# Merging the attention stage and the feed-forward stage of the first block into one hand-ordered stage

## The chip, the cores and the metric

The program runs on one core of one Trainium2 chip. The metric is device time in microseconds (us) from start to end of one launch, on the slowest core, which here is the only one; lower is better. The core has five engines that run beside each other, each with a queue that is worked off in order: TensorE (PE; its weight loads are shown as PEld), VectorE (DVE), ScalarE (ACT), GpSimd (POOL) and SyncE (SP), which issues most of the transfers. TensorE writes to PSUM, eight banks of 128x512 fp32; the others read PSUM or SBUF, except GpSimd, which here works on SBUF alone. An instruction that needs a result of another engine waits for a semaphore, and what is queued behind it waits too.

## What is computed

The reference is a chain of four blocks on x of shape 16x256x128, each with an attention part and a feed-forward part, both wrapped in a norm before, a norm after, and a residual sum. The change touches the first block only, and the norm that starts the second:

```
x = x + layernorm(L0_attn(layernorm(x)))
x = x + layernorm(L0_ffn(layernorm(x)))
...   # the second block starts from layernorm(x)

def L0_attn(x):            # Wq, Wk: 128x32, one head
    score = (x @ Wq) @ (x @ Wk).T / sqrt(32)
    score = where(tril, score, 0);  score = where(score != 0, score, float32.min)
    return softmax(score) @ (x @ (Wvdown @ Wvup))

def L0_ffn(x):             # int weights / 127, hidden width 384
    return (silu(x @ wg.T) * (x @ wu.T)) @ wd.T
```

A score that is exactly zero is masked as well, not only one above the diagonal. The layernorm here has no gain or bias: (x - mean) / sqrt(var + 1e-5).

## The kernel before

**Tiling.** The 16 sequences of 256 tokens are cut into eight groups of two sequences. A group's tokens lie in one tile of 128 partitions by four column blocks (NT = 4) by 128 features; x[g], for g from 0 to 7, stays in SBUF throughout. Matmuls need features on the partitions, so a normed tile is transposed by TensorE, four 128x128 blocks into one PSUM bank (`transposed`, L311), and copied to SBUF. All matmuls of this block are fp32; each appears in the trace as two records.

**Norms.** `stats` (L260, L262) gives mean and variance of four token blocks on VectorE; GpSimd turns the variance into 1/sqrt (L249 a scale and sum, L250 a power); `normed` (L269) applies both on VectorE, four instructions of 128x128. `residual` norms y in this way and adds it to x on GpSimd (L289).

**The attention stage** `stage_l0_attn` (L550 on) makes, per group: norm, transposes, q and k (L322, copied out by `k.copy`, which alternates between VectorE, L242, and ScalarE, L244), values, and per sequence b the scores of 256 queries by 256 keys in one bank. VectorE then multiplies by a 0/1 causal mask (L581), marks zeros with -2^100 (L583), adds the marks (L584), takes the row maximum, negated (L586), and scales it (L587). ScalarE takes the exponential with that maximum as bias and gives the row sum (L592). TensorE transposes the weights (L602), ScalarE copies them (L604), TensorE multiplies by the values, and VectorE divides by the sums (L605, L612). The result is normed and added to x.

**The feed-forward stage** `stage_l0_ffn` (L621 on) starts when the attention stage has issued all its groups. It converts the integer weights (L627), and per group makes norm, transposes, and for three blocks of 128 hidden units a gate matmul, an up matmul, a silu on ScalarE (L643) and a product on VectorE (L644); then the down matmuls, the residual, and the norm of the new x into z[g], which the second block reads.

**What sets the order.** Both stages are Python generators, woven by `interleave`: three groups at a time, a new one every four steps, in the attention stage; four at a time, every three steps, in the other. The framework's scheduler then reorders the instructions of these stages within their queues. `turns` (L378 on) is another weave, used by later stages: each item has a starting turn and moves one step per turn (up to three when it is behind), and under `manual_schedule` the queues keep the order of the source. PSUM is given out in rings by tag: `BANKS` has four rings of two banks each ("mm", "s", "o", "t"); later stages use one large ring.

**Loads.** All loads are issued on SP in the order of the source, each taking some 0.43 us to issue: x of group 0, the identity, x of groups 1 and 2, the attention weights with the causal mask (256 KB), the other x, fourteen constants, the feed-forward weights, the next block's weights.

Of the kernel before, what the change touches and what calls it, by code (L numbers as in the profile page):

```python
# [31 lines left out]

BANKS = {"mm": 2, "s": 2, "o": 2, "t": 2}
MAMBA_BANKS = {"s": 6, "o": 2, "mm": "s", "t": "s"}
RING_BANKS = {"s": 7, "o": 1, "mm": "s", "t": "s"}
NEG = -(2.0**100)

# [68 lines left out]
    return c  # L106


def causal01():

    q = np.arange(SEQ).reshape(2, P).T
    return (np.arange(SEQ)[None, None, :] <= q[:, :, None]).astype(np.float32)


def packs(i):

    out = {"const": constants(), "att": attention_constants()}
    a = out["l0"] = Pack()
    a.add("wq", i["L0_attn_Wq"])
    a.add("wk", i["L0_attn_Wk"])  # L120
    a.add("causal", causal01())
    a = out["l0v"] = Pack()
    a.add("down", i["L0_attn_Wvdown"].T)
    a.add("up", i["L0_attn_Wvup"])
# [66 lines left out]
def idle(n):  # L191

    for _ in range(n):
        yield


def bc(ap, axis, n):

    ap = ap.unsqueeze(axis)
    shape = list(ap.shape)  # L200
    shape[axis] = n
    return ap.to_broadcast(shape)
# [343 lines left out]
        return out  # L546


def stage_l0_attn(k, x, w, wv):
    nc, v = k.nc, k.nc.vector  # L550
    scale = 1.0 / math.sqrt(32.0)
    ps = k.ps("mm")
    k.mm(ps[:, :D], wv["down"], wv["up"])
    wfull = k.t([P, D], "wfull", 1)
    v.tensor_copy(wfull, ps[:, :D])

    def group(g):
        xn = yield from k.norm(x[g], "xn", 3)
        yield
        xT = k.transposed(xn, "xT", 3)  # L560
        yield
        qk = []
        for name in ("wq", "wk"):
            ps = k.ps("mm")
            k.mm(ps[:32, :], w[name], xT)
            t = k.t([32, GT], name + "T", 3)
            k.copy(t, ps[:32, :])
            qk.append(t)
        yield
        val = k.tokens(xT, wfull, "v", 3)  # L570
        es, sms = [], []
        for b in range(2):
            keys = slice(b * SEQ, (b + 1) * SEQ)
            s = k.ps("s")
            for t in range(2):
                q = qk[0][:, (2 * b + t) * P : (2 * b + t + 1) * P]
                k.mm(s[:, t * SEQ : (t + 1) * SEQ], q, qk[1][:, keys])


            sc = k.t([P, 512], "sc", 4)  # L580
            v.tensor_tensor(sc, s, w["causal"], ALU.mult)  # L581
            z = k.t([P, 512], "z", 2)
            v.tensor_scalar(z, sc, 0.0, NEG, ALU.is_equal, ALU.mult)  # L583
            v.tensor_tensor(sc, sc, z, ALU.add)  # L584
            nm = k.t([P, 2], "nm", 6)
            v.tensor_reduce(nm, sc.rearrange("p (t n) -> p t n", t=2), AX.X, ALU.max, negate=True)  # L586
            v.tensor_scalar(nm, nm, scale, None, ALU.mult)  # L587
            e = k.t([P, 512], "e", 4)
            sm = k.t([P, 2], "sm", 6)
            for t in range(2):  # L590
                sl = slice(t * SEQ, (t + 1) * SEQ)
                nc.scalar.activation(  # L592
                    e[:, sl], sc[:, sl], AF.Exp, bias=nm[:, t : t + 1], scale=scale, accum_out=sm[:, t : t + 1]
                )
            es.append(e)
            sms.append(sm)
            yield
        o = k.t([P, NT, D], "o", 3)
        for b in range(2):
            tp = k.ps("t")  # L600
            for j in range(4):
                nc.tensor.transpose(tp[:, j * P : (j + 1) * P], es[b][:, j * P : (j + 1) * P], k.c["ident"])  # L602
            eT = k.t([P, 512], "eT", 3)
            nc.scalar.copy(eT, tp)  # L604
            v.reciprocal(sms[b], sms[b])  # L605
            yield
            ps = k.ps("o")
            for t in range(2):
                for kb in range(2):
                    at = (2 * t + kb) * P  # L610
                    k.mm(ps[:, t * D : (t + 1) * D], eT[:, at : at + P], val[:, 2 * b + kb, :], kb == 0, kb == 1)
            v.tensor_tensor(  # L612
                o[:, 2 * b : 2 * b + 2, :], ps[:, : 2 * D].rearrange("p (t d) -> p t d", t=2), bc(sms[b], 2, D), ALU.mult
            )
            yield
        yield from k.residual(x[g], o)

    k.interleave([group(g) for g in range(NG)], 3, 4)


def stage_l0_ffn(k, x, w, then):  # L621

    v = k.nc.vector
    f = {}
    for name in ("gate", "up", "down"):
        f[name] = k.t([P, 384], "f_" + name, 1)
        v.tensor_scalar(f[name], w[name], float(np.float32(1.0 / 127.0)), None, ALU.mult)  # L627
    down = f["down"].rearrange("p (c n) -> p c n", c=3)

    def group(g):  # L630
        xn = yield from k.norm(x[g], "xn", 3)
        yield
        xT = k.transposed(xn, "xT", 3)
        yield
        h = k.t([P, 3, GT], "h", 3)
        for c in range(3):
            cols = slice(c * P, (c + 1) * P)
            gt = k.ps("s")
            k.mm(gt, f["gate"][:, cols], xT)
            u = k.ps("mm")  # L640
            k.mm(u, f["up"][:, cols], xT)
            sg = k.t([P, GT], "sg", 3)
            k.nc.scalar.activation(sg, gt, AF.Silu)  # L643
            v.tensor_tensor(h[:, c, :], u, sg, ALU.mult)  # L644
            yield
        y = k.tokens(h, down, "y", 3)
        yield
        yield from k.residual(x[g], y)
        yield
        yield from then(g)  # L650

    k.interleave([group(g) for g in range(NG)], 4, 3)


def stage_l1_attn(k, x, ws, rows, z, then):
# [1043 lines left out]
def program(ctx: ExitStack, tc: tile.TileContext, xin, dram, at, out):  # L1699
# [12 lines left out]
    def load(p, name, only=None, dt=F32):  # L1712

        got = {}
        for n, (a, width) in at[name].items():
            if only is not None and n not in only:
                continue
            src = dram[name][:, a : a + width]
            t = p.tile([src.shape[0], width], dt, tag=f"{name}_{n}", name=f"{name}_{n}")
            nc.sync.dma_start(out=t, in_=src)  # L1720
            got[n] = t
        return got
# [11 lines left out]
    for g in range(NG):  # L1734
        nc.sync.dma_start(out=x[g], in_=xin[2 * g : 2 * g + 2].rearrange("b (t p) d -> p (b t) d", p=P))
        if g == 0:
            const = load(base, "const", {"ident"})
        elif g == 2:
            l0, l0v = load(p0, "l0"), load(p0, "l0v")
    const.update(load(base, "const", set(at["const"]) - {"ident"}))  # L1740
    k = Ctx(tc, const, None, None)
    k.load = load
    k.mhalf = base.tile([P, P], F32, tag="mhalf", name="mhalf")
# [10 lines left out]
    def stage(name, side, fn, *args, banks=BANKS):  # L1754
        with phase(name, banks, side):
            fn(k, x, *args)

    l0f = load(p0, "l0f", dt=I32)
    pa = opened("wa", "left")
    l1 = [load(pa, f"l1_{i}") for i in range(4)]  # L1760
    k.dram = ctx.enter_context(tc.tile_pool(name="spill", bufs=1, space=bass.MemoryType.DRAM))
    pz = opened("z", "left")
    z = [pz.tile([P, NT, D], F32, tag=f"z{g}", name=f"z{g}") for g in range(NG)]
    stage("l0a", "left", stage_l0_attn, l0, l0v)
    stage("l0f", "left", stage_l0_ffn, l0f, lambda g: k.norm_to(z[g], x[g]))
    closed("w0")
    l2 = load(opened("wb", "right"), "l2")
    psoft = opened("soft", "right")
# [57 lines left out]
```

## Time and profile before

| | |
|---|---|
| median of 3 runs | 3084.61 us (3083.8 to 3086.37) |
| profiled execution, its own time | 3086.15 us |
| its span in the trace | 3084.4 us |
| mean granted TensorE clock | 0.944 |
| busy over the span | PE 2781.1 (90%), PEld 1871.6 (61%), DVE 2038.4 (66%), ACT 1540.9 (50%), POOL 1000.8 (32%) |
| first transposes of the attention stage | 9.37 us |
| first gate matmul of the feed-forward stage | 144.0 us |
| last down matmuls | until 225.15 us |
| first transposes of the second block | 242.8 us |

The first block is thus some 8% of the span. The profile page cuts the span into 40 slices of 77 us and gives the busy share of each in tenths; the first block is the first three of them, in which PE shows 7, 7, 8 and the granted clock 7, 6, 9, while most later slices show PE at 9. A busy PE is not PE at its peak: matmuls are pipelined, and a matmul at a lower granted clock is busy for longer. For throughput one reads how far the starts of successive matmuls lie apart. Durations of single instructions are read from the groups of instructions (busy time and mean of one) and the timeline (instructions in order of time, merged when alike, with the idle time before them and what ended it). Idle time of an engine that is not the bottleneck costs nothing.

### The profile page before, as it was taken

Reading aid. Unit: us, or ns where it says so; the run is one execution under the profiler, and the core shown is the slowest. Engines: PE = TensorE matmul, PEld = TensorE weight load, DVE = VectorE, ACT = ScalarE, POOL = GpSimd, SP = SyncE. Lnnn points to the kernel's source line nnn. Section 1 sums busy time; section 2 is a strip of 40 time slices with the busy share of each in tenths; the row PEclk is TensorE's granted clock in tenths of the full one; section 3 lists DMA queues with packets and bytes.
Section 4 is the critical chain, followed back from the end, with each engine's and each line's share of the span. In section 5 each row is a group of like instructions: output and inputs, shape, how many; then the busy total and the mean of one; then the engine's idle time right before and its main releaser. Section 6 shows DMA issues by size and latency. Waiting matters only on the chain. (4 is left out here: it accounts for less than half of the span.)

```text
span 3084.4 us, 58954 instructions
## 1 busy us (share of the span) xinstructions
PE 2781.1 (90%) x23500; PEld 1871.6 (61%) x23500; DVE 2038.4 (66%) x5480; ACT 1540.9 (50%) x3237; POOL 1000.8 (32%) x1318
## 2 busy tenths in 40 slices
PE   7788999999999599999968999799999699978798
PEld 4445677777777488888853444466666344435576
DVE  6677656465566889899866774566665577637442
ACT  2224645555555467677634666344443277742222
POOL 1244333333335400000033555422232466553232
PEclk7698999999999799999988999899999799989899
DMA  3000000000000000000010000000000000010000
GB/s 100 25 1 1 2 1 2 1 1 1 1 2 18 19 8 8 12 12 8 8 45 27 2 1 1 1 1 1 1 1 1 1 1 1 1 55 1 1 15 15
DMA packets 29291, 31.52 MB, mean 10 GB/s; under 512 B 7308, under 2 KB 20172, under 8 KB 28876
## 3 DMA queue, kind: packets, MB, share of 16 engines
q1 hardware_dynamic: 29016, 27.76, 3.0%
q8 instruction: 185, 3.03, 0.4%
q14 instruction: 90, 0.74, 0.1%
HBM read 23.55 MB, written 4.19 MB: 9 GB/s over the span
## 5 line engine op out<-in xcount | busy, mean ns | idle before, releaser
L249 POOL TENSOR_SCALAR ln_rs<-ln_mv 128x4 f32<-128x4 f32 x192 | 39.5, 206 | 923.5 <-DVE ln_mv L262 812.5
L445 DVE TENSOR_REDUCE at_nm<-ps_s 128x2 f32<-128x512 f32 (+1 forms) x384 | 238.2, 682 | 123.1 <-PE ps_s L322 123.1
L477 ACT ACTIVATE at_e<-ps_s 128x512 f32<-128x512 f32 x384 | 198.1, 604 | 93.4 <-PE ps_s L322 91.2
L1311 DVE TENSOR_TENSOR scan<-ps_s,lm 128x384 f32<-128x384 f32 x256 | 124.7, 550 | 143.1 <-PE ps_s L322 142.8
L483 POOL TENSOR_SCALAR_AFFINE_SELECT at_e<-at_e 128x1024 f32<-128x1024 f32 (+1 forms) x96 | 135.1, 1408 | 215.8 <-ACT at_e L477 215.5
L250 POOL TENSOR_TENSOR ln_rs<-ln_rs,mhalf 128x4 f32<-128x4 f32 x192 | 194.6, 1015 | 15.1
L774 DVE TENSOR_REDUCE l_max<-ps_s 128x3 f32<-128x384 f32 x256 | 124.1, 549 | 64.0 <-PE ps_s L322 64.0
L322 PE MATMUL ps_o<-my,meT 128*128 128x129 f32 x1024 | 145.2, 289 | 19.5 <-ACT mgot L1068 17.0
L322 PEld LDWEIGHTS ps_s<-l_w,mlp_h 128*128 128x128 f32 x1280 | 149.4, 192 | 18.8 <-issue 15.1
L322 PE MATMUL ps_s<-l1f_phi,mxT 128*128 128x256 f32 x512 | 141.5, 399 | 16.4 <-DVE mpart L930 16.4
L322 PEld LDWEIGHTS ps_o<-my,meT 128*128 128x128 f32 x1024 | 128.7, 196 | 37.8 <-ACT mgot L1068 22.6
L322 PE MATMUL ps_s<-km,qT 32*128 32x512 f32 x768 | 140.2, 661 | 12.1 <-POOL km L369 10.7
L322 PE MATMUL ps_s<-l_w,mlp_h 128*128 128x128 f32 x1280 | 150.2, 275 | 0.3
L322 PE MATMUL ps_s<-qm,kT 32*128 32x512 f32 x768 | 144.1, 656 | 5.2 <-DVE at_nm L445 5.0
L824 POOL TENSOR_SCALAR_AFFINE_SELECT e<-e 128x512 f32<-128x512 f32 x128 | 78.6, 635 | 178.5 <-ACT e L821 178.5
L322 PE MATMUL ps_o<-at_e,at_vm 128*32 128x128 f32 (+1 forms) x2048 | 122.6, 336 | 15.2 <-ACT at_oT L507 15.2
L322 PE MATMUL ps_mm<-mdisp,mxn 128*128 128x128 f32 x1024 | 128.0, 282 | 4.6 <-DVE mdisp L968 4.5
L322 PEld LDWEIGHTS ps_mm<-mdisp,mxn 128*128 128x128 f32 x1024 | 124.4, 198 | 7.5 <-DVE mdisp L968 6.2
L821 ACT ACTIVATE e<-ps_s 128x384 f32<-128x384 f32 x256 | 105.6, 513 | 39.7 <-PE ps_s L322 39.6
L322 PE MATMUL ps_s<-xT,l_w 128*128 128x512 f32 x256 | 119.3, 596 | 2.7 <-ACT mlp_h L709 2.7
L1049 ACT ACTIVATE lg<-lg,mless 128x256 f32<-128x256 f32 x256 | 116.4, 523 | 0.0
L322 PEld LDWEIGHTS <-b_ident 128*128 128x128 bf16 x640 | 49.8, 98 | 108.8 <-issue 98.9
(418 smaller groups left out, 6978.9 us busy)
## 6 DMA issues: line engine op xcount, KB each, us to landing
mw<-in_l1fw SPq DMA_DIRECT2D x16, 256.0 KB, 2.6
moe_w<-in_moe SPq DMA_DIRECT2D x16, 256.0 KB, 5.3
l_w<-in_l SPq DMA_DIRECT2D x10, 256.0 KB, 3.2
x<-in_x SPq DMA_DIRECT2D x8, 256.0 KB, 4.1
xs<-x SPq DMA_DIRECT2D x8, 256.0 KB, 2.0
slT<-xs SPq DMA_DIRECT2D x8, 256.0 KB, 2.6
out<-x SPq DMA_DIRECT2D x8, 256.0 KB, 2.3
l1f_phi<-in_l1f SPq DMA_DIRECT2D x1, 1024.0 KB, 6.8
```

The source lines that it names most:

```text
L249: g.tensor_scalar(out, in_, scale, eps, ALU.mult, ALU.add)
L250: g.tensor_tensor(out, out, self.mhalf[:, :n], ALU.pow)
L322: self.nc.tensor.matmul(out, lhsT=lhsT, rhs=rhs, start=start, stop=stop, skip_group_check=True)
L445: v_.tensor_reduce(nm[:, t, r, vs], s, AX.X, ALU.max, negate=True)
L477: nc.scalar.activation(e[:, r], s, AF.Exp)
L483: nc.gpsimd.affine_select(at, at, [[0, 4], [0, n], [1, P]], ALU.is_ge, 0.0, base=0, channel_multiplier=-1)
L774: v.tensor_reduce(mx[:, b, :, h, 16], s, AX.X, ALU.max, negate=True)
L821: nc.scalar.activation(e[:, h].rearrange("p j n -> p (j n)"), s[:, : 3 * P], AF.Exp)
L824: nc.gpsimd.affine_select(e[:, :, j, :], e[:, :, j, :], [[0, 4], [1, P]], ALU.is_ge, 0.0, base=0, channel_multiplier=-1)
L1049: nc.scalar.activation(at, at, AF.Exp, bias=less[n][:, t, b : b + 1])
L1311: v.tensor_tensor(m, s[:, : SEQ + P], lm[:, SCAN_HEADS[4 * (t // 2) + 2 * i + hh], :], ALU.mult)
```

## The change

The two stages become one, `stage_l0`, in which all eight groups are woven by `turns` under `manual_schedule`: group g starts at turn 4g, and each has 28 turns from the first statistics to the norm into z. Some turns are left empty (`idle(2)`) behind the statistics. Further:

- The causal mask is added in PSUM by TensorE: a bf16 identity times a bf16 tile of 0 and -2^100 starts the bank, and the score matmuls add to it. The 256 KB mask is no longer loaded.
- The marks for zero scores are made from PSUM, and one instruction per 256 columns adds them, negates the sum and takes the minimum, which is the negated maximum. The exponential's scale gets the opposite sign.
- The norms before the attention part, before the feed-forward part and into z are applied by ScalarE as scale and bias; GpSimd makes the bias, two small instructions. The two norms of residuals stay on VectorE, now in place.
- All PSUM copies go to ScalarE; the copies of constants and the conversions of weights run as an item of their own beside group 0.
- PSUM is one ring of eight banks.
- The attention weights and the constant negmask are loaded directly behind the identity, the feed-forward weights behind x of group 2.

```diff
+ONE_RING = {"s": 8, "mm": "s", "t": "s"}
...
-    a.add("causal", causal01())
...
+def stage_l0(k, x, w, wv, wi, z):
...
+    def constants():
+        full = k.t([P, P], "negs", 1)
+        gp.memset(full, NEG)
+        gp.memset(negs[:, 2, :], 0.0)
+        yield
+        nc.scalar.copy(negs[:, 1, :], full)
+        nc.scalar.copy(ident, k.c["ident"])
+        ps = k.ps("s")
+        k.mm(ps[:, :D], wv["down"], wv["up"])
+        nc.scalar.copy(wfull, ps[:, :D])
+        for t in (0, 3):
+            nc.scalar.copy(negs[:, t, :], k.c["negmask"])
+        yield from idle(8)
+        for name in f:
+            v.tensor_scalar(f[name], wi[name], float(np.float32(1.0 / 127.0)), None, ALU.mult)
+            yield
+    def stats(src):
+        mv, rs = k.stats(src)
+        nb = k.t([P, NT], "ln_nb", 6)
+        gp.tensor_scalar(nb, mv[:, :, 0], -1.0, None, ALU.mult)
+        gp.tensor_tensor(nb, nb, rs, ALU.mult)
+        return nb, rs
+    def normed(out, src, nb, rs):
+        for t in range(NT):
+            nc.scalar.activation(
+                out[:, t, :], src[:, t, :], AF.Identity, bias=nb[:, t : t + 1], scale=rs[:, t : t + 1]
+            )
...
+    def scores(qk, b):
+        s = k.ps("s")
+        k.mm(s, ident, negs, True, False)
+        for t in range(2):
+            q = qk[0][:, (2 * b + t) * P : (2 * b + t + 1) * P]
+            k.mm(s[:, t * SEQ : (t + 1) * SEQ], q, qk[1][:, b * SEQ : (b + 1) * SEQ], False, t == 1)
+        return s
+    def masked(s):
+        zero = k.t([P, 512], "zero", 2)
+        v.tensor_scalar(zero, s, 0.0, NEG, ALU.is_equal, ALU.mult)
+        sc = k.t([P, 512], "sc", 4)
+        nm = k.t([P, 2], "nm", 6)
+        for t in range(2):
+            sl = slice(t * SEQ, (t + 1) * SEQ)
+            v.tensor_tensor_reduce(
+                out=sc[:, sl], in0=s[:, sl], in1=zero[:, sl], scale=-1.0, scalar=3.0e38,
+                op0=ALU.add, op1=ALU.min, accum_out=nm[:, t : t + 1],
+            )
+        v.tensor_scalar(nm, nm, scale, None, ALU.mult)
+        return sc, nm
...
     def group(g):
+        nb, rs = stats(x[g])
+        yield from idle(2)
+        xn = k.t([P, NT, D], "xn", 2)
+        normed(xn, x[g], nb, rs)
+        yield
+        xT = by_feature(xn, "xT")
+        yield
...
+        s0 = scores(qk, 0)
+        ps = k.tokens_ps(xT, wfull)
+        val = k.t([P, NT, D], "v", 3)
+        nc.scalar.copy(val, ps)
+        yield
+        got0 = masked(s0)
+        s1 = scores(qk, 1)
+        yield
+        e0, sm0 = weights(*got0)
+        got1 = masked(s1)
+        yield
+        e1, sm1 = weights(*got1)
+        eT0 = weights_T(e0)
+        yield
+        o0 = product(eT0, val, 0)
+        eT1 = weights_T(e1)
+        yield
+        o = k.t([P, NT, D], "o", 3)
+        divided(o, o0, sm0, 0)
+        o1 = product(eT1, val, 1)
+        yield
+        divided(o, o1, sm1, 1)
+        mv, rs = k.stats(o)
+        yield from idle(2)
+        k.normed(o, o, mv, rs)
+        gp.tensor_tensor(x[g], x[g], o, ALU.add)
+        yield
...
+        for cs in ((0, 1), (2,)):
+            for c, u, sg in todo:
+                v.tensor_tensor(h[:, c, :], u, sg, ALU.mult)
+            todo = []
+            for c in cs:
+                cols = slice(c * P, (c + 1) * P)
+                gt = k.ps("s")
+                k.mm(gt, f["gate"][:, cols], xT)
+                u = k.ps("s")
+                k.mm(u, f["up"][:, cols], xT)
+                sg = k.t([P, GT], "sg", 4)
+                nc.scalar.activation(sg, gt, AF.Silu)
+                todo.append((c, u, sg))
             yield
...
+        nb, rs = stats(x[g])
+        yield from idle(2)
+        normed(z[g], x[g], nb, rs)
+        yield
+    with k.tc.manual_schedule():
+        k.turns([(0, group(0)), (0, constants())] + [(4 * g, group(g)) for g in range(1, NG)])
...
-    stage("l0a", "left", stage_l0_attn, l0, l0v)
-    stage("l0f", "left", stage_l0_ffn, l0f, lambda g: k.norm_to(z[g], x[g]))
+    stage("l0", "left", stage_l0, l0, l0v, l0f, z, banks=ONE_RING)
```

## The prediction

> **What bounds the kernel now.** The change touches only the start of the program, so I read the windows of that start first, cut where the stages change hands: up to the first scores, the attention stage (L550), the seam, the feed-forward stage (L621), its last products, the seam to the next block, and, to compare, a stretch of that next block.
>
> ```profile
> core 0: us, PE busy (x) PEld busy (x) DVE busy (x) ACT busy (x) POOL busy (x), PEclk, DMA share, GB/s
> 0.00:16.90 16.90, 6.71 (x18) 2.73 (x18) 7.97 (x39) 1.86 (x2) 4.00 (x11) 1.00 0.72 185
> 16.90:122.40 105.50, 84.02 (x344) 54.33 (x344) 74.21 (x251) 31.34 (x85) 20.69 (x28) 0.72 0.17 44
> 122.40:144.00 21.60, 7.91 (x31) 5.78 (x29) 13.40 (x57) 3.25 (x10) 6.15 (x8) 0.55 0.13 35
> 144.00:218.70 74.70, 67.82 (x288) 39.90 (x289) 58.16 (x252) 19.11 (x31) 30.49 (x44) 0.97 0.05 16
> 218.70:225.20 6.50, 4.83 (x29) 3.48 (x27) 4.22 (x21) 0.61 (x2) 2.97 (x5) 1.00 0.00 0
> 225.20:242.80 17.60, 0.00 (x0) 0.01 (x1) 10.42 (x59) 0.57 (x1) 11.03 (x23) 0.64 0.00 0
> 260.00:380.00 120.00, 117.64 (x1267) 82.28 (x1266) 79.81 (x273) 69.20 (x175) 41.45 (x60) 1.00 0.01 2
> ```
>
> Columns: stretch, its length, busy us and instructions of each engine, granted clock, DMA. The next block keeps TensorE at 117.6 of 120 us and clock 1.00. The attention stage has it at 84 of 105.5 at 0.72, the seam at 8 of 21.6 at 0.55, and for 17.6 us before the next block it does nothing. No engine is full anywhere before 144 us: that part is bound by chains and by a slow clock. The waits between 20 and 225 us name the chains:
>
> ```profile
> ACT sg L643 <- PE ps_s L322: 47.2, 22, 5.2
> ...
> ACT e L592 <- DVE nm L587: 34.9, 8, 4.5
> PEld ps_t L602 <- ACT e L592: 24.4, 10, 4.2
> ...
> PE ps_t L602 <- ACT e L592: 20.6, 8, 3.6
> ACT eT L604 <- PE ps_t L602: 19.3, 14, 2.1
> ```
>
> Per batch: scores, five VectorE passes, exponential, transposes, copy, product, with three groups in flight; whoever is next waits. So there is time to win, about 242.8 us down to what the busiest engine needs. The prices of single instructions:
>
> ```profile
> 205.85 1.02 PE L322 MATMUL ps_s<-xT,f_gate 128*128 128x512 f32 x2
> ...
> 212.86 2.39 PE L322 MATMUL ps_mm<-f_down,h 128*128 128x128 f32 x20
> ...
> 251.27 0.28 ACT L753 ACTIVATE kr<-ps_s 128x128 f32<-128x128 f32 x1 [1.79 <-DVE q L752]
> ...
> 251.55 1.28 ACT L754 ACT_TABLE_LOAD   x1
> ...
> 252.85 0.28 ACT L754 ACTIVATE ke<-ps_s 128x128 f32<-128x128 f32 x1
> ```
>
> Gate matmul, 128x512 fp32, two records: the next starts 0.86 us later (205.85 after 204.99), at clock 1.00. Twenty records of 128 columns take 2.39 us, 0.12 each. The table load takes 1.28 us, and the next activation starts 0.02 us after it.
>
> **What one group costs after the change.** TensorE, clock 1.00: 16 transposes at 0.11 (four in 0.60 at 256.08, the last one's 0.27 included) 1.8; q and k 2x0.86 = 1.7; values 8x0.12 = 0.95; scores 8 records of 256 columns, half a 512 record each, 1.7; products 16x0.12 = 1.9; gate and up 6x0.86 = 5.15; down 24x0.12 = 2.9: **16.1 us**. The mask adds two bf16 matmuls of 512 columns; the row b_negmask by b_ident has four of 256 in 0.61, so about 0.25 each: **16.6**.
>
> ScalarE has 12 activations of 128x128 with two per-row operands per group, which no row shows. Bounds from:
>
> ```profile
> L592 ACT ACTIVATE e<-sc,nm 128x256 f32<-128x256 f32 x32 | 16.0, 501 | 34.9 <-DVE nm L587 34.9
> L696 ACT ACTIVATE xT<-ps_s,l_ln_b,l_ln_g 128x512 f32<-128x512 f32 x15 | 11.7, 781 | 33.5 <-PE ps_s L311 33.5
> ...
> L733 ACT ACTIVATE qT<-ps_s 128x512 f32<-128x512 f32 x8 | 4.8, 597 | 15.3 <-PE ps_s L322 15.3
> L753 ACT ACTIVATE kr<-ps_s 128x128 f32<-128x128 f32 x16 | 4.5, 279 | 8.5 <-DVE q L752 8.0
> ```
>
> Two such operands cost 781-597 = 184 ns over the plain 512-wide one; kr, 128 wide and plain, is 279; an SBUF source adds 83 (L779 454 against L795 371). That is 0.55 at most; L592 is 45 ns under the same sum, and back-to-back exps start 0.40 after each other, 0.10 less than they last. I take 0.40 a piece, 1.7 per norm of four; the ends are 0.8 (the 128-wide PSUM copies near 253 us start 0.15 apart) and 2.2. ScalarE: 3 norms 5.1, 8 copies at 0.58 4.6 (three of them from VectorE, L242), 4 exps 2.0, 3 silus 1.8, and table loads. Exponential and silu now alternate: in the instruction order, which is fixed before the run, twelve loads stand in the stage, where before had two; two per full period, 2.6. Sum **16.1 us**.
>
> **A rule against the change** is in the Trainium skill, "ScalarE: Activation LUTs", section "Table sets: the hidden batching unit": do all work of one table set before the next; its section "What ACT_TABLE_LOAD costs" puts each switch at about 2.66 us, 1.28 load and 1.38 drain. The trace shows the 1.28 and no drain behind it (251.55 + 1.28, next at 252.85). By the row a period pays 2.6, by the rule 5.3, which would make ScalarE the bound at 18.8. I take the row, since the trace has this very switch.
>
> VectorE: 5 statistics at 1.15 (L260, L262) 5.75; two norms 2.2; mask 2x1.85; two divisions 1.1; three h 2.0: **14.8 us**. The mask part replaces 2.6 us of five operations per batch (L581 to L587) by: one scan of PSUM, 0.69 (as L1124, a 512-wide one from PSUM); two fused add-and-minimum of 256, not in the trace, at 0.42 (L612) plus an accumulator read; 0.15. The read I put at 0.08 of pace (ScalarE's 0.19 one adds 0.1). The ends for one fused instruction are 0.42 and 0.85 (two passes). GpSimd: five 1.3, three scale-times-mean pairs 0.4, two adds 1.27: 10.2, never the bound, but each norm's chain grows by 0.4.
>
> **The period.** A group starts every four turns and has 28 (0 to 27). Following the queues from the down product: TensorE does down, transposes, product, scores, values (6.8 us), gate and up of two blocks (10.2), product and scores (12.3), third gate at 13.2. ScalarE, busy with values, load, two silus and two norms till then, goes on at 13.4: silu 0.6, load 1.28, two exps 1.0, copy of xT 0.6, 16.9. Only then come q and k, 1.7, and the next down: **18.7 us** with the hops. This loop ends last, not a full engine; VectorE's 14.8 lies beside it. The eight-bank ring hides too: an allocation meets one eight earlier, read in the turn before.
>
> **The sum.** What the turns of one group hold (T, S, V, G for TensorE, ScalarE, VectorE, GpSimd): 0 statistics V 1.15, G 1.7; 2 norm S 1.7; 3 transposes T 0.45, S 0.6; 4 q and k T 1.7, S 1.15; 5 scores, values T 2.05, S 0.6; 6 mask V 1.85, scores T 1.1; 7 exps S 1.0, mask V 1.85; 8 exps, transposes S 1.6, T 0.45; 9 product, transposes T 1.4, S 0.6; 10 product T 0.95, V 0.55; 11 V 1.7, G 1.3; 13 norm V 1.1, add G 1.27; 14 as 0; 16 norm S 1.7; 17 as 3; 18 T 3.45, S 2.5; 19 T 1.7, V 1.4, S 0.6; 20 V 0.7; 21 down T 2.9, S 0.6; 22 V 1.15, G 1.3; 24 as 13; 25 as 0; 27 norm S 1.7. A turn costs the largest sum over the groups in it, or its longest chain.
>
> Up to turn 3 (xT of group 0) I keep before's 11.4 us (L242, 10.71 + 0.68). The norm's input comes earlier, since GpSimd's power no longer stands behind two other groups (7.91), but ScalarE first has six constant copies, of which those of wfull and negmask await DMA. Turns 4 to 16 hold attention only: 2.0 to 4.5 each, 39.8 together, plus 3 for a clock still near 0.7: 54.2. Turns 17 to 35 are 4.75 periods of 18.7: 89, to 143. Turns 36 to 49 drain, 2.3 to 4.8 each, 43.4 to the last down product at **186.4**. From there to the next block's first transpose stays 17.6: copy, statistics, norm, add, statistics are the same, and GpSimd's 0.4 more is met by VectorE no longer doing the last norm. 204 against 242.8: **38.8 us less**. Behind it the order of every compute queue is unchanged.
>
> Moved or dropped at no cost: SP's 256 KB causal load goes, negmask and the three feed-forward weights rise past 8 to 19 issues of 0.43; x of groups 1 and 2 are issued some 2.4 us later, needed from 12 us on; the next blocks' loads swap their order and come sooner than at 139 us. The seam of 9 idle us at 133 goes; the weight conversions (3x0.36) run beside.
>
> The span is 3084.4, the profiled run 3086.15, the median 3084.61: span minus 38.8 is 3045.6, the same for the median **3046**.
>
> **Rivals.**
> 1. TensorE itself binds (0.17): period 16.6, and fill and drain overlap more (38 and 36): 11.4+38+79+36+17.6 = 182, 3024. For it: the next block at 98%. Against: the feed-forward stage needs 8.5 per group by the same prices and took about 10.
> 2. The queues go in lockstep (0.15): each turn costs its fullest engine, 4.5+6.8+5.5+4.9 = 21.7 a full period, 101.5 for turns 17 to 35; with 8 for the slow clock 11.4+39.8+8+101.5+43.4+17.6 = 222, 3063; with drains by the rule or fused passes of 0.85 some 6 more. For it: strict order, so one late instruction holds its queue.
> 3. **Slower** (0.06): the clock stays where the attention stage and seam had it. TensorE then needs 16.6/c a period; 54.2+43.4+17.6 leave 127.6 for 4.75 periods at the break with 242.8: 26.9 each, c = 0.62. At 0.55 it is 30.2, +16: 3100. For it: 0.72 and 0.55 in the windows, while the chains leave TensorE waiting for the table switch. Against: the feed-forward stage, at 85% of its price, had 0.97.
> 4. It doesn't do what it says (0.01), and nothing moves: against it, the fixed order weaves the groups as written.
>
> The forecast has 0.61, with 3034 to 3058 as its own range (period 17.5 to 20, drain 38 to 46). To hold 8 in 10 I take 3027 to 3068. A measurement here tells about 0.2% (6 us) from no change: faster 0.93, same 0.01, slower 0.06.
>
> **What would show it.** Right: next block's first transpose near 204 us; full periods of 18 to 19.5 (start to start of a group's f_down products); two table loads of 1.28 in each; clock above 0.9 from 60 to 140 us; q and k waiting for ScalarE's xT. Wrong: norms over 0.5 apart or fused passes over 0.6, VectorE or ScalarE full, a clock under 0.8 in the full periods, or the time after the stage changed by over 3 us.

## The result, and the profile after

| | before | after |
|---|---|---|
| median | 3085.49 us (3083.8 to 3087.92, 4 executions) | 3031.27 us (3029.9 to 3032.37, 4 executions) |
| ratio | | 0.9823 (95% interval 0.9806 to 0.984) |
| span of the profiled execution | 3084.4 us | 3029.1 us |
| first transposes of the second block | 242.8 us | 187.73 us |
| span behind that mark | 2841.6 us | 2841.4 us |

The kernel is 54.2 us faster, 1.8%; 38.8 were forecast. All of it lies ahead of the mark, that is, ahead of the first transposes of the second block; behind it nothing moved. (One execution of a kernel further down, the one with the mask on VectorE, took 8860 us where its three others took 3030 to 3032; its ratio leaves it out, and its cause is not known.) The windows of the changed kernel: up to the first xT, the start with attention only (and first feed-forward work), up to the first down product, three full periods and a fourth in which no new group begins, the drain to the end of the last down product, and the tail up to the mark:

```profile
core 0: us, PE busy (x) PEld busy (x) DVE busy (x) ACT busy (x) POOL busy (x), PEclk, DMA share, GB/s
0.00:10.80 10.80, 2.39 (x6) 1.22 (x6) 2.30 (x16) 4.48 (x11) 3.96 (x15) 1.00 0.67 188
10.80:52.00 41.20, 39.31 (x171) 20.96 (x172) 24.21 (x120) 26.13 (x65) 13.24 (x26) 0.96 0.60 159
52.00:61.00 9.00, 7.61 (x31) 3.57 (x29) 6.83 (x31) 7.03 (x17) 3.48 (x7) 1.00 0.01 3
61.00:137.00 76.00, 70.03 (x366) 45.47 (x366) 50.98 (x250) 57.18 (x124) 34.17 (x61) 1.00 0.04 11
137.00:170.10 33.10, 29.75 (x153) 19.90 (x151) 21.81 (x104) 19.13 (x42) 19.57 (x34) 1.00 0.00 0
170.10:187.73 17.63, 0.00 (x1) 0.03 (x1) 8.29 (x51) 3.88 (x9) 11.97 (x27) 0.63 0.00 1
```

Where the attention stage of before had TensorE at 84 of 105.5 us and a clock of 0.72, the start now has it at 39.3 of 41.2 at 0.96, and the periods at 70 of 76 at 1.00. The seam is gone; the idle tail has stayed, 17.63 us. All that lies ahead of the mark, first before, then after:

```profile
0.00:242.80 242.80, 171.29 (x706) 106.23 (x707) 168.38 (x675) 56.74 (x130) 75.33 (x118) 0.81 0.15 40
```

```profile
0.00:187.73 187.73, 149.09 (x723) 91.16 (x723) 114.42 (x570) 117.81 (x265) 86.39 (x168) 0.96 0.19 51
```

TensorE does the same matmuls and the mask products on top, and yet is busy for 22.2 us less, at a granted clock of 0.96 instead of 0.81; 32.9 us less it stands still. The gain is thus more than the waits that went. Of the waits between 20 and 190 us, those at the exponential:

```profile
PEld ps_s L629 <- ACT e L621: 11.8, 16, 2.6
...
ACT e L621 <- DVE nm L613: 0.7, 1, 0.7
```

The old kernel waited 34.9 us for the row maxima (L592 <- L587); now ScalarE's exponentials wait less than 1 us for them, and TensorE waits for the exponentials. Why, two stretches of one full period show. First TensorE's queue, from the third gate product on, then ScalarE's from the third silu on (start, length, engine, line, operation, idle time before it and what ended it):

```profile
92.82 1.12 PE L316 MATMUL ps_s<-xfT,f_gate 128*128 128x512 f32 x2
93.78 1.02 PE L316 MATMUL ps_s<-xfT,f_up 128*128 128x512 f32 x2
94.64 0.60 PE L305 MATMUL ps_s<-const_ident,xn 128*128 128x128 f32 x4
96.55 0.93 PE L629 MATMUL ps_s<-const_ident,e 128*128 128x128 f32 x4 [1.30 <-ACT e L621]
97.51 1.05 PE L316 MATMUL ps_s<-xT,l_wq 128*32 128x512 f32 x2
98.39 1.02 PE L316 MATMUL ps_s<-xT,l_wk 128*32 128x512 f32 x2
```

```profile
93.98 0.60 ACT L710 ACTIVATE sg<-ps_s 128x512 f32<-128x512 f32 x1 [0.35 <-PE ps_s L316]
94.60 1.28 ACT L621 ACT_TABLE_LOAD   x1
95.90 0.51 ACT L621 ACTIVATE e<-sc,nm 128x256 f32<-128x256 f32 x1
...
96.89 0.56 ACT L589 COPY xT<-ps_s 128x512 f32<-128x512 f32 x1
```

Third gate, silu, table load, two exponentials, copy of xT, q: that is the loop of the prediction. TensorE stands still for 1.30 us while ScalarE changes its table and takes the first exponential, and q starts 0.06 us after the copy of xT ends. From down product to down product a full period takes 19.12 us, three times over (starts at 61.10, 80.22, 99.34, 118.47); the next, without the transposes, q and k of a new group, takes 17.09.

### The profile page after: what moved, and what is told of

The parts are those of the page before. It is cut to its first block, busy times and chain, and to the rows that moved or that the text cites. A ratio compares the mean times of both kernels' runs of the same rounds, so it can differ in the third digit from the quotient of the medians.

```text
span 3029.1 us, 59064 instructions
## 1 busy us (share of the span) xinstructions
PE 2758.7 (91%) x23516; PEld 1855.1 (61%) x23516; DVE 1984.5 (66%) x5375; ACT 1602.5 (53%) x3372; POOL 1013.6 (33%) x1368
## 5 line engine op out<-in xcount | busy, mean ns | idle before, releaser
L316 PEld LDWEIGHTS ps_s<-l_w,mlp_h 128*128 128x128 f32 x1280 | 149.4, 192 | 18.8 <-issue 15.1
L316 PE MATMUL ps_s<-l1f_phi,mxT 128*128 128x256 f32 x512 | 141.4, 398 | 16.9 <-DVE mpart L1009 16.7
L900 ACT ACTIVATE e<-ps_s 128x384 f32<-128x384 f32 x256 | 105.5, 510 | 39.7 <-PE ps_s L316 39.6
L1367 ACT COPY BT<-ps_s 128x512 f32<-128x512 f32 x64 | 37.5, 586 | 154.6 <-PE ps_s L316 154.6
```

Source lines behind the costliest of these rows:

```text
L316: self.nc.tensor.matmul(out, lhsT=lhsT, rhs=rhs, start=start, stop=stop, skip_group_check=True)
L900: nc.scalar.activation(e[:, h].rearrange("p j n -> p (j n)"), s[:, : 3 * P], AF.Exp)
L1367: nc.scalar.copy(s, ps)
```

## The experiments

Each kernel is the changed one with the edit shown; `...` marks lines left out. The code behind the stage is the same in all, and its part of the span lay between 2833.4 and 2842.9 us, differing with the chip and the execution. So beside the time stand the length of a full period (start to start of the down products) and the mark, the first transposes of the second block.

| kernel | median us | before, same chip | ratio (95%) | full period us | mark us |
|---|---|---|---|---|---|
| changed kernel | 3031.27 | 3085.49 | 0.9823 (0.9806 to 0.984) | 19.12 | 187.73 |
| silu left out | 3020.85 | 3083.48 | 0.9796 (0.9779 to 0.9812) | 17.70 | 183.07 |
| heads first | 3032.65 | 3083.48 | 0.9838 (0.9823 to 0.9852) | 18.1 to 19.2 | 195.50 |
| silu by tanh | 3051.56 | 3083.48 | 0.9897 (0.9882 to 0.9911) | 19.5 to 22.1 | 212.19 |
| five turns | 3065.10 | 3083.48 | 0.9942 (0.9927 to 0.9956) | 23.0 to 24.3 | 229.06 |
| norms on VectorE | 3026.21 | 3084.65 | 0.9812 (0.9797 to 0.9827) | 19.12 | 184.49 |
| mask on VectorE | 3032.09 | 3084.65 | 0.9825 (0.9806 to 0.9845) | 18.75 | 191.85 |
| all old operations | 3063.52 | 3084.65 | 0.9934 (0.9919 to 0.9948) | 18.7 to 23.4 | 222.73 |
| two stages | 3048.73 | 3084.65 | 0.9884 (0.9869 to 0.9898) | 9.6 and 9.93 | 205.77 |
| late heads, norms on VectorE | 3023.13 | 3081.12 | 0.9813 (0.9799 to 0.9828) | 17.4 to 17.7 | 181.80 |
| copies alternating | 3039.47 | 3081.12 | 0.9862 (0.9848 to 0.9877) | 19.12 | 196.25 |
| no fixed order | 3044.45 | 3081.12 | 0.9884 (0.9868 to 0.9901) | 19.3 to 21.4 | 202.69 |
| three turns | 3018.25 | 3081.12 | 0.9794 (0.9779 to 0.9808) | 17.94 | 182.81 |

### What sets the period

**Silu left out.**

```diff
-                nc.scalar.activation(sg, gt, AF.Silu)
+                nc.scalar.activation(sg, gt, AF.Identity)
```

> The changed kernel with the silu left out: ScalarE copies the gate with the identity function, in the same place and for the same 512 columns, so that exponential and silu no longer alternate and the stage needs no table switch behind its first. Loop theory (the full period of 19.1 us is set by third gate, silu, table load, two exponentials, copy of xT, q and k): the load of 1.28 us leaves the loop and the copy of xT is no longer late, full periods 17.0 to 17.9 us, the next block's transposes 6 to 11 us earlier, time 3020 to 3026 us. TensorE theory (TensorE alone binds, table loads cost nothing): periods stay within 0.3 of 19.1, time 3028 to 3034 us.

This kernel leaves out the silu, so it does not compute the block. The table loads are gone, and with them the wait of TensorE; the same place in this kernel's trace:

```profile
94.08 0.60 PE L305 MATMUL ps_s<-const_ident,xn 128*128 128x128 f32 x4
94.56 0.93 PE L629 MATMUL ps_s<-const_ident,e 128*128 128x128 f32 x4
95.52 1.05 PE L316 MATMUL ps_s<-xT,l_wq 128*32 128x512 f32 x2
```

The transposes of the exponentials follow those of xn after 0.48 us instead of 1.91. The period falls by 1.42 us, the 1.30 of the wait and a little. (The mark comes 4.7 us sooner and not 6 to 11, since the second group's start was 2.9 us later; why, the last section tells.) The loop theory holds, and what remains, 17.70, is nearly TensorE's own: busy 52.54 of 53.09 us over three periods.

**Heads first.** The first five turns of each group stand ahead in each turn, so that the copy of xT passes the third silu and the load.

```diff
-        k.turns([(0, group(0)), (0, constants())] + [(4 * g, group(g)) for g in range(1, NG)])
...
+        k.turns(
+            [(4 * g, head(g)) for g in range(NG)] + [(0, constants())]
+            + [(4 * g + 5, rest(g)) for g in range(NG)]
+        )
```

> The changed kernel with the first five turns of every group (statistics, norm, transposes, q and k) put ahead of the other groups within a turn; nothing is left out and the number of table loads stays at twelve. Loop theory: the copy of xT now stands before the third silu and the load, q and k no longer wait for it, the load falls beside up, q and k of TensorE; periods 17.0 to 17.9 us, the next block's transposes 6 to 10 us earlier, time 3021 to 3026 us. ScalarE theory (the loads cost ScalarE's own time, wherever they stand): periods stay near 19.1, time 3028 to 3034 us. TensorE theory: no change either.

A miss in time. ScalarE's queue in this kernel:

```profile
120.37 0.59 ACT L589 COPY xT<-ps_s 128x512 f32<-128x512 f32 x1 [1.66 <-PE ps_s L305]
120.85 1.65 ACT L582 ACTIVATE z<-x,ln_nb,ln_rs 128x128 f32<-128x128 f32 x4
122.40 0.57 ACT L714 ACTIVATE sg<-ps_s 128x512 f32<-128x512 f32 x1
122.99 1.28 ACT L621 ACT_TABLE_LOAD   x1
```

The edit did more than it was meant to: the norm into z, which had filled the gap ahead of the third gate, now stands behind a copy that waits 1.66 us for TensorE, and pushes the silu and the load back. The attention-only start got longer too: the fourth group's transposes are at 46.36 us instead of 40.40, half of that from the slower first matmuls of the last section. So this run does not decide; the next does.

**Late heads, norms on VectorE.** The same from group 4 on, where feed-forward work meets the heads, and with no norm on ScalarE that could stand in between. Beside the edit of "norms on VectorE" below:

```diff
+        k.turns(
+            [(4 * g, head(g)) for g in range(4, NG)] + [(0, whole(0)), (0, constants())]
+            + [(4 * g, whole(g)) for g in range(1, 4)] + [(4 * g + 5, rest(g)) for g in range(4, NG)]
+        )
```

> The three norms on VectorE, and from group 4 on the first five turns of a group (statistics, norm, transposes, q and k) ahead of the other groups within a turn, so that in full periods ScalarE's queue reads: two silus, copy of xT, third silu, table load, two exponentials, copies of q and k. No norm of ScalarE stands between the copy of xT and the third silu now. Loop theory: q and k run beside the load, only the transposes of the exponentials wait, by 0.2 us or less; full periods 17.6 to 18.1 us, table loads still twelve; 4 to 5 us less than with the norms on VectorE alone, time 3019 to 3024 us. Theory that the loads cost their time wherever they stand: periods 19.1, time 3025 to 3029 us.

```profile
109.67 0.60 ACT L706 ACTIVATE sg<-ps_s 128x512 f32<-128x512 f32 x1 [0.33 <-PE ps_s L316]
110.28 1.28 ACT L613 ACT_TABLE_LOAD   x1
```

```profile
110.36 1.05 PE L316 MATMUL ps_s<-xT,l_wq 128*32 128x512 f32 x2
111.25 1.02 PE L316 MATMUL ps_s<-xT,l_wk 128*32 128x512 f32 x2
112.24 0.93 PE L621 MATMUL ps_s<-const_ident,e 128*128 128x128 f32 x4
113.00 2.84 PE L316 MATMUL ps_s<-f_down,h 128*128 128x128 f32 x24
```

The load is still there, as long as before, but q and k now run beside it: TensorE is busy for 52.41 of 52.57 us, and the period is 17.4 to 17.7. In this kernel, then, a load costs what stands behind it on the path, not its own 1.28. Against norms on VectorE alone the mark comes 2.7 us sooner: three periods save 1.6 each, and the first down product is 2.2 us later (60.43 against 58.19). The ratios of the two kernels do not tell them apart.

**Silu by tanh**, which needs no switch.

```diff
-                nc.scalar.activation(sg, gt, AF.Silu)
+                nc.scalar.activation(sg, gt, AF.Tanh, scale=0.5)
+                v.scalar_tensor_tensor(sg, sg, 1.0, gt, ALU.add, ALU.mult)
...   # the factor 0.5 goes into the down weights
```

> The changed kernel with silu(g) computed as half of (tanh(g/2) + 1) times g: the hyperbolic tangent shares a table with the exponential, so the switches go, and VectorE gets one more pass over 512 columns of PSUM per block of hidden units, three of about 0.7 us a group (14.8 to about 16.9 us of VectorE per period). The half is folded into the down weights. Loop theory: as without silu if VectorE stays beside, periods 17 to 18 us, time 3020 to 3028 us. VectorE theory (with two more us VectorE becomes the bound, or its pass stands in the chain from gate to down): periods 19 or more, time 3030 to 3040 us.

Slower by more than either side said. VectorE is not full, 15.0 of 22.0 us; its queue in one period:

```profile
92.21 0.69 DVE L712 SCALAR_TENSOR_TENSOR sg<-sg,ps_s 128x512 f32<-128x512 f32 x1 [3.85 <-ACT sg L711]
93.92 0.69 DVE L712 SCALAR_TENSOR_TENSOR sg<-sg,ps_s 128x512 f32<-128x512 f32 x1 [1.03 <-ACT sg L711]
```

The new pass waits at the head of the queue for the tanh, in the very turn of the gate product, with statistics, division and mask behind it. Later the third product h comes behind all of these, and down waits 2.5 us for it. By this reading strict order made the pass dear, not its length; a kernel with the pass a turn later, which would show it, was not run.

**Five turns and three turns** between groups; nothing else differs (the diff shows five).

```diff
-            [(4 * g, group(g)) for g in range(1, NG)]
+            [(5 * g, group(g)) for g in range(1, NG)]
```

> The changed kernel with a group every five turns instead of four; every instruction the same, only the weave is wider. In the order on ScalarE this makes four table loads in a full period instead of two (one silu turn now lies between two exponential turns). Loop theory: two more loads of 1.28 us on the chain of each of seven periods, time 9 to 18 us longer, 3040 to 3049 us. Theory that the turn pattern does not count because queues run ahead over turns and TensorE's sum sets the pace: within 3 us of 3031.

> The changed kernel with a group every three turns; nothing else differs. The copy of xT falls in the turn of the first silus, one turn ahead of the exponentials, so q and k no longer stand behind the table load; nine loads in the stage. Loop theory: periods 17 to 18.3 us, a shorter start, time 3020 to 3029 us. Buffer theory (nine groups in flight wait for each other's tiles of two to four buffers): periods of 19 or more, 3032 to 3045 us.

With five, the direction was right and the size less than half of what came, 34 us of time and 41 at the mark. The stage has 24 loads instead of 12, which is the 15 us that the expectation counted. But TensorE now waits twice in a period, 4.6 us instead of 1.3: in the second line for weights behind two loads, and in the first, which the expectation had not seen, for the copy of xfT, which stands behind two norms of ScalarE (four activations each). TensorE is also busy for longer, 19.6 us a period instead of 17.7, at a granted clock of 0.93.

```profile
94.53 1.12 PE L316 MATMUL ps_s<-xfT,f_gate 128*128 128x512 f32 x2 [1.68 <-ACT xfT L589]
...
103.75 2.08 PE L316 MATMUL ps_s<-v,eT 128*128 128x128 f32 x8 [2.92 <-ACT eT L631]
```

With three, q and k stand a turn ahead of the load, the period is 17.94 (TensorE 35.20 of 35.88 us), and the mark is 182.81 us although its first matmuls ran at half pace for longer (below). It is the fastest of those that compute the block: ratio 0.9794 (0.9779 to 0.9808) against 0.9823 (0.9806 to 0.984). The intervals just touch, and of the 8.7 us between the two gains only 4.9 lie ahead of the mark; the period is what shows the gain. The time is 1.8 us under the loop theory's range; the buffers that its rival feared did not bind.

### Where the gain comes from

**Norms on VectorE**, as before the change.

```diff
-        gp.tensor_scalar(nb, mv[:, :, 0], -1.0, None, ALU.mult)
-        gp.tensor_tensor(nb, nb, rs, ALU.mult)
...
-    def normed(out, src, nb, rs):
-        for t in range(NT):
-            nc.scalar.activation(
-                out[:, t, :], src[:, t, :], AF.Identity, bias=nb[:, t : t + 1], scale=rs[:, t : t + 1]
-            )
+    def normed(out, src, mv, rs):
+        k.normed(out, src, mv, rs)
```

> The changed kernel with the three norms applied by VectorE again, as before the change (four instructions of 0.28 us each, subtract and multiply; GpSimd's two bias instructions go). Order theory (the gain is the dense order of TensorE): VectorE goes from 13.4 to about 16.7 us per period of 19.1 and stays beside, ScalarE gets 4.9 us of air; the loop through the table load is untouched; time within 8 us of the changed kernel, 3028 to 3039 us. Operations theory (cheaper work on VectorE carries the gain): some 3.3 us on each of seven to eight groups, 3050 us or more.

The move to ScalarE earned nothing: the periods are 19.12 with and without it, and undoing it brings the mark 3.2 us forward and the time to 3026.21, 1.8 under the order theory's range. The two ends show it without the pace of the first matmuls, which also differs between the two kernels. Here the tail, first of the changed kernel, GpSimd and ScalarE, then of this one, VectorE:

```profile
177.40 1.02 POOL L244 TENSOR_TENSOR ln_rs<-ln_rs,mhalf 128x4 f32<-128x4 f32 x1
178.40 0.23 POOL L576 TENSOR_SCALAR ln_nb<-ln_mv 128x4 f32<-128x4 f32 x1
178.71 0.20 POOL L577 TENSOR_TENSOR ln_nb<-ln_nb,ln_rs 128x4 f32<-128x4 f32 x1
```

```profile
178.95 1.65 ACT L582 ACTIVATE z<-x,ln_nb,ln_rs 128x128 f32<-128x128 f32 x4 [5.96 <-POOL ln_nb L577]
```

```profile
176.24 1.11 DVE L263 TENSOR_SCALAR z<-x,ln_mv,ln_rs 128x128 f32<-128x128 f32 x4 [1.42 <-POOL ln_rs L244]
```

Two bias instructions, 0.51 us, and four activations at 1.65 instead of 1.11: 1.0 us longer where the chain is bare. At the start xT of group 0 is copied by 8.59 instead of 10.80 us, since it waits neither for that nor for ScalarE's constants: 2.2 us.

**Mask on VectorE**: no mask product, five VectorE operations, the 256 KB mask loaded.

```diff
-        k.mm(s, ident, negs, True, False)
...
+        v.tensor_tensor(sc, s, w["causal"], ALU.mult)
+        v.tensor_scalar(zero, sc, 0.0, NEG, ALU.is_equal, ALU.mult)
+        v.tensor_tensor(sc, sc, zero, ALU.add)
+        v.tensor_reduce(nm, sc.rearrange("p (t n) -> p t n", t=2), AX.X, ALU.max, negate=True)
```

> The changed kernel with the causal mask as before: no mask by TensorE, five VectorE operations per batch (product with a loaded 0/1 mask, marks, sum, maximum, scale; 2.6 us against 1.7), the 256 KB mask loaded again behind negmask. Order theory: TensorE 0.6 us less per period, VectorE 1.8 more (15.2 of 19.1), no change of the loop; time 3028 to 3037 us. Operations theory: the longer chain from scores to exponentials makes each exponential late, by about 1 us per batch and sixteen batches, 3043 us or more.

The time is the changed kernel's within what can be told. The periods are shorter by 0.37: without the mask product in between, the scores start 0.2 us sooner, twice a group (0.53 instead of 0.75 us after the start of the matmul ahead of them, and 0.99 instead of 1.20). The start is longer by 5.6 (first down at 66.69 us), part of it through the half pace of TensorE. In the full periods the longer chain is hidden.

**Copies alternating** between VectorE and ScalarE (six a group, `k.copy` for `nc.scalar.copy`), and **all old operations**: these copies, norms and mask together, in the new order.

> The changed kernel with the PSUM copies alternating between VectorE and ScalarE as before the change, all else as changed. VectorE 13.4 + about 2.4 us per period of 19.1. Sum theory (the old operations together cost 32 us because together they fill VectorE, not one by one): within 10 us of the changed kernel, 3030 to 3041 us. Copy theory (a copy behind VectorE's norms and masks is late by itself, and TensorE waits for it): 3045 us or more.

> The changed kernel's one stage and its order of the source, but with the operations of before: mask on VectorE, three norms on VectorE, PSUM copies alternating between VectorE and ScalarE. VectorE then has 13.4 + 3.3 + 1.8 + about 2.5 of copies = 21 us per group. Order theory: VectorE sets the period at 21 to 22.5 instead of 19.1, over about five full periods and with a somewhat longer start and end: 3041 to 3055 us, so over half of the 54 us stays. Operations theory: the weave alone brings little, 3070 us or more.

Copies alone cost 8.5 us at the mark, none of it in the period and most in the start (first down product at 68.25 us instead of 61.10). Together the three cost 35.0 at the mark and 32 in time, though alone they come to −3.2 + 4.1 + 8.5 = 9.4. The window of the full periods, with all old operations:

```profile
76.00:160.00 84.00, 70.88 (x342) 46.71 (x340) 74.09 (x283) 35.54 (x70) 29.37 (x41) 0.96 0.00 1
```

VectorE is at 74 of 84 us, and two of its periods, 22.3 and 23.4 us, are near what the expectation worked out (21 to 22.5). The total lies 8 above its range, since the start took 16 us longer as well (first down at 76.77). So of the 54 us the new order keeps only 21 with these operations, not over half: the expectation of the order theory failed there, and that of the operations theory (3070 or more) did not come true either.

**Two stages**: the same operations and a fixed order, first all attention, then all feed-forward.

```diff
+    def forward(g):
         nb, rs = stats(x[g])
...
+        k.turns([(4 * g, forward(g)) for g in range(NG)])
```

> The changed kernel's operations in two stages after one another, both in the order of the source with a group every four turns: all eight groups' attention, then all eight groups' feed-forward part; table loads fall from twelve to two. Merge theory: attention alone at about 10.2 us a group (its pace in the first 40 us of the changed kernel), to xT of the last group at 82 and its end at about 112; then feed-forward at 8.5 to 9.5 us a group, first down at about 120 and last at 190; next block at 205 to 212, time 3047 to 3055 us. Rival (a dense order within each stage is enough, and sparing ten table loads pays for the seam): next block at 185 to 192, time 3028 to 3035 us.

`forward` is the second half of `group`, from the norm into xf on. As the merge theory had it. A group takes 9.6 us in attention and 9.93 in feed-forward, 19.5 together, so the merged period of 19.12 is hardly better: there the loop ate what the overlap offered (late heads shows 17.5). What merging saves in the changed kernel is, by this, the second drain and fill. The seam in this kernel:

```profile
91.63 1.58 PE L316 MATMUL ps_s<-v,eT 128*128 128x128 f32 x8 [2.90 <-ACT eT L631]
93.00 1.06 PE L629 MATMUL ps_s<-const_ident,e 128*128 128x128 f32 x4
94.79 2.08 PE L316 MATMUL ps_s<-v,eT 128*128 128x128 f32 x8 [0.73 <-ACT eT L631]
104.77 1.63 PE L305 MATMUL ps_s<-const_ident,xf 128*128 128x128 f32 x4 [7.90 <-ACT xf L582]
```

**No fixed order**: the framework orders the merged stage.

```diff
-    with k.tc.manual_schedule():
-        k.turns(...)
+    k.turns(...)
```

> The changed kernel's stage with every operation and the same turns, but without the fixed order: the framework's scheduler orders the instructions of the stage in their queues. It puts 22 table loads into the stage instead of 12. Order theory (the order of the source carries much of the gain): ten more loads of 1.28 us, most of them on the chain, and matmuls of one group cut in two by those of another: 3045 to 3065 us. Rival (merging is what counts, who orders does not): within 5 us of 3031.

Fifteen us of the mark. ScalarE has 21 switches between silu and exponential instead of 11, and the period grows to 21.4; the time, 3044.45, is just under the range of the order theory. How much of this is the switches and how much the order of the matmuls is not separated.

Undone one at a time, order (15.0), merge (18.0) and operations (35.0) come to 68 us, more than the 55.1 of the mark: each counts partly for what another also removes. Before to two stages is 37.0 without any merging; this is the fixed order and the new operations together, which no run separates in two stages.

## Why the prediction was right, and where its sizes were off

The direction, the mechanism and the wide range (3027 to 3068) held; the forecast was 15 us too slow, and its own range (3034 to 3058) was missed by 2.7. Of the signs it gave, the period, the two loads, the clock and q behind the copy of xT came; the mark at 204 and a drain of 38 to 46 did not. Its sum, term by term against the trace:

| term | forecast us | measured us |
|---|---|---|
| xT of group 0 | 11.4 | 10.80 |
| turns 4 to 16, attention only | 42.8 | 33.0 (to 43.81) |
| turns 17 to 35, full periods | 89 | 91.0 (to 134.79) |
| turns 36 to 49, drain | 43.4 | 35.3 (to 170.1) |
| tail | 17.6 | 17.63 |
| mark | 204 | 187.73 |

**Right.** The period: 18.7 forecast, 19.12 measured, by the loop that was named; third silu at 13.4 us behind the down product (13.76 here), q at 16.9 (17.29). Silu left out and late heads show that this loop and nothing else holds it above 17.4 to 17.7. A little luck is in it: the third gate starts at 12.60 instead of 13.2, but the silu 1.16 us after it instead of 0.2, and the two nearly cancel. The price of a switch: 1.28 us and the next activation 0.02 later, eleven times in the stage, as the row said. The rule of 2.66 us (the Trainium skill, "ScalarE: Activation LUTs", section "What ACT_TABLE_LOAD costs") would by the forecast's sum have made ScalarE the bound at 18.8; it is busy for 15.18 of 19.12. The norms: four in 1.65, forecast 1.7. The fused passes: 0.42 each and a read of 0.08 (L609), as taken, which kept VectorE beside, at 13.37 of 19.12:

```profile
L582 ACT ACTIVATE xf<-x,ln_nb,ln_rs 128x128 f32<-128x128 f32 x32 | 13.2, 485 | 0.0
...
L609 DVE CUSTOM_DVE_ANT_0 sc<-ps_s,zero 128x256 f32<-128x256 f32 x32 | 12.3, 422 | 0.6
```

The tail, and that nothing behind the mark moves, came as forecast too.

**Mis-sized: the attention-only turns and the drain**, 9.8 and 8.1 us, which is more than the whole miss; the periods' 2.0 give some back. The rule "a turn costs the largest sum over the groups in it, or its longest chain" treats a turn as a barrier. It is only an order: each queue goes on into the next turn as soon as its operands are there, so VectorE's costly turn can lie beside TensorE's costly turn of another number. What counts over several turns is each engine's sum over all of them, and TensorE's is the largest; it is busy for 39.3 of the 41.2 us of the start and 29.75 of the 33.1 of the drain. This is read from the busy shares; no run tests it by itself. Nor is the sum alone the answer: by the forecast's table of turns TensorE has 23.7 us of work in turns 4 to 16, 26.7 with the 3 for the clock, and 31.2 in the drain, which is 6.3 and 4.1 too little. The measured times lie between the two rules, nearer to the engine's sum. In full periods the loop was followed along the queues, not turn by turn, and there the sum was good.

The 3 us for a slow clock were about what came, though the windows show 0.96: q and k of the first two groups run at half pace (last section) and take 3.52 and 3.48 us from q to the next matmul, where 1.83 is the full pace, 3.3 us together. So all of the 9.8, and a little more, is in the turns.

**Mis-sized too, without harm: TensorE's 16.6 us a group.** It is busy for 17.73 of the 19.12, and with the loop out of the way a period takes 17.4 to 17.7. The largest single error is the scores, taken as half a 512 record each, 1.7 for eight; the trace of before has the eight, in its first group:

```profile
16.93 2.21 PE L322 MATMUL ps_s<-wkT,wqT 32*128 32x256 f32 x8
```

So the loop stands only some 1.5 us above TensorE, not 2.1.

**The rivals.** TensorE alone had the drain right and the start nearer (36 and 38 forecast, 35.3 and 33.0 measured) and the period wrong (16.6). Its total, 3024, is nearer to the measured time than the forecast's 3046, but by luck: its start was 5 us too long and its periods 12 us too short (79 for 91.0). Lockstep had the period wrong by 2.6 us and the clock rival the clock.

**Costed at nothing, and not nothing:** the norms' move. The prediction named the longer GpSimd chain and set it against VectorE's relief; in the full periods it is hidden, at the two ends it costs 2.2 and 1.0 us.

## What to carry to other kernels

A fixed order in turns is not a barrier: price the full period by the loop through the queues, and take start and drain to lie between the busiest engine's sum and the sum of the turns, here nearer to the former. A table switch cost here only what was queued behind it and due, so moving a copy ahead of it was worth as much as removing it (17.4 to 17.7 against 17.70), and a change of the number of turns between groups can do it with no edit to the work. Single operations moved off an engine that is not full earned little each (undone one at a time, norms, mask and copies move the mark by -3.2, 4.1 and 8.5 us, and no period gets longer), yet together they kept it from filling (35.0); what is moved at the bare ends of a stage is paid in full.

## What was not expected of the hardware

TensorE's first matmuls run at half pace, and when that ends differs between executions that begin with the same instructions. The first scores of four 256-column records take 1.13 us in one profile and 2.07 in another, first in the changed kernel, then in the one with three turns:

```profile
15.10 1.13 PE L316 MATMUL ps_s<-wkT,wqT 32*128 32x256 f32 x4 [0.34 <-ACT wkT L660]
```

```profile
15.20 2.07 PE L316 MATMUL ps_s<-wkT,wqT 32*128 32x256 f32 x4
```

In the second the pace is full only from about 26 us on, and the second group's transposes come at 21.63 instead of 18.51 us. Silu left out, heads first and mask on VectorE show the same. The granted clock of the window from 15 to 20 us reads 1.00 in both; the durations tell it. The changed kernel falls back once more: q and k of its second group, from 20.98 to 24.46 us, are again about 1.7 us apart instead of 0.9, and there the granted clock reads 0.66 (20 to 25 us).

The pace can halve behind a wait too, and does not always. In silu by tanh the same 20 records of the down product, behind the same wait:

```profile
82.43 4.12 PE L316 MATMUL ps_s<-f_down,h 128*128 128x128 f32 x20 [2.51 <-DVE h L716]
...
104.57 2.50 PE L316 MATMUL ps_s<-f_down,h 128*128 128x128 f32 x20 [2.52 <-DVE h L716]
```

So a wait can cost more than its length. What decides it stays open. The mark of a single profile is therefore uncertain by about 3 us, and 3 us between two kernels are safe only where the periods show them.
